# ScalarE evaluates to the end of a unit, and the last group gets all PSUM banks and both engines

## The chip, the cores and the metric

The kernel runs on one core of one Trainium2 chip. The time is the device time of one launch, in microseconds (us). Before the change it was 7317.06 us, the median of three runs (7311.98 to 7319.36); the profiled execution spans 7306.6 us.

The engines are called PE (TensorE, matrix products; PEld is its weight load), DVE (VectorE), ACT (ScalarE), POOL (GpSimd) and SP (SyncE, which here issues nearly all transfers). A matrix product goes into PSUM, in tiles of 128 x 512 fp32 values, and DVE or ACT takes it out; that is called an eviction here.

## The reference

The input `x` is 16 images of 32 channels, 128 x 128. Four residual layers follow each other, each on a group normalisation `_gn` of its input:

```python
x = x + L0(gn(x))    # a diagonal LSTM over the image
x = x + L1(gn(x))    # an adder convolution on quantised values
x = x + L2(gn(x))    # Hartley modes: transform, mix 32 x 32 modes, transform back
x = x + L3(gn(x))    # an edge-detecting encoder and decoder, multiplied with its input
```

Layer 1 is the one of the unit stage. With 8-bit quantised input `qx` and weights `qw` (3 x 3, 32 channels in and out) it computes a sum of absolute differences:

```python
patches = conv_general_dilated_patches(qx, (3, 3), (1, 1), [(1, 1), (1, 1)])
out = lax.map(lambda wk: -jnp.sum(jnp.abs(pr - wk[None, :, None]), axis=1), wf)
```

Layer 3 is the one of the end. Five edge operators are normalised over the image; then come conv1 (3 x 3, 160 to 32 channels), pooling to 64 x 64, conv2, pooling to 32 x 32, conv3, pooling to 16 x 16, conv4, and three steps of "upsample by 2, then 3 x 3 convolution" back to 128 x 128; the result is multiplied with the layer's input.

## The kernel before

**Three parts.** `stage0` does layer 0. `rest` (L438) does all others: class `Differences` does layer 1 for each image, class `After` does layers 2 and 3 in groups of four images (0 to 3). Work of `After` on images that are ready is woven into the loop of `Differences`. What is left of it when that loop ends, and the whole of group 3, runs in `drain` (L403).

**The unit.** `Differences.run` (L610) goes over 32 units: 16 images, two halves of 64 rows. The identity |a - b| = 2 max(a - b, 0) - (a - b) splits a unit into 72 evaluations of max(q - w, 0), one for each pair of a weight slot and a tap, over 128 partitions x 8192 values (8320 where the tap needs no shift), and a linear part (`linear`, L594). An evaluation is one instruction, on DVE (L684, into `d_dve`, three buffers) or on ACT (L681, into `d_act`, two buffers). PE then sums each result with 16 matrix products (`sums`, L581, products in L586) into four accumulators `acc1`, each a PSUM tile.

**Which engine evaluates.** For each evaluation the loop keeps planned times in `weave`: DVE_US = 2.36, ACT_US = 7.15. It computes when DVE and when ACT would end the evaluation, given their buffers, and takes ACT if that is at most 0.5 later than DVE. The last four evaluations of a unit, `i >= 68`, are always DVE's.

**The end of a unit.** At `i == 71` all sums not yet issued are issued. In the next unit the accumulators are replaced only after two DVE evaluations have been put in: then `finish` (L563) empties the old four (four instructions of L567, with the residual added, four of statistics, L569), and the new unit's sums may start. Four PSUM tiles belong to the units and four to the woven work.

**The woven work.** `After.work` is a generator. It yields planned PE time, and `Weave.advance` lets it run in PE's gaps up to the time when the next sum is due. Evictions and transfers that come later are put off by `later` and run when planned time has passed. In the loop of `Differences` the written order is kept on each engine (`keep_order`). In `drain` it isn't: the framework's scheduler orders the instructions there, by their written order and its own view of what is ready.

**The drain.** Two weaves run: the one that still has the rest of group 2, and one for group 3. The one with the smaller planned time goes next. Each has a pool of four PSUM tiles, `b_ps` and `c_ps`. When group 2 is done, group 3 goes on alone, with its four tiles.

**A round.** In `After` a round is a set of four accumulators (`acc`, L904), the products into all four, and four evictions. `spread` (L1539) writes an eviction as four instructions for 32 partitions each (`blk` counts the accumulators), all on the engine that its caller names: DVE for the pooled layers, conv4 and the first upsampling, ACT for conv1's output and the second upsampling. Lines: conv1 L1607, conv2 to conv4 L1455, upsampling L822 with edge terms in L847.

**The last layer.** `last` (L1652) goes over four units of 32 rows, two rounds each: DVE makes `s` (L1735) and multiplies it with the residual `xr` (L1698, two buffers), ACT subtracts a mean (`done`, L1708), then four transfers store the unit (L1714) and four reload `xr` for the unit after the next (L1677). The store is put off by 14 planned us, the reload by 10 more.

Of the kernel before, what the change touches and what calls it, by code (L numbers as in the profile page):

```python
# [7 lines left out]
F32 = mybir.dt.float32  # L8
# [291 lines left out]
class Weave:  # L300
# [10 lines left out]
    def __init__(self, work):  # L311
        self.work, self.pending = work, None
        self.pe = self.dve = self.act = self.now = self.base = 0.0
        self.until = self.ready = 0.0
        self.draining = False
        self.finished, self.count, self.put_off, self.for_act, self.ends = -1, 0, [], [], {}

    def later(self, us, step):
# [84 lines left out]
def drain(*weaves):  # L403

    live = list(weaves)
    for w in live:
        w.draining = True
    while live:
        w = min(live, key=lambda w: w.now)
        us = w.step()  # L410
        w.now = max(w.now + (us or 0.0), w.until)
        w.due(float("inf") if us is None else w.now)
        if us is None:
            live.remove(w)


def keep_order(nc, tc, start):
# [13 lines left out]


DVE_US, ACT_US, PE_US = 2.36, 7.15, 1.0
SLACK, CLOCK = 3.0, 1.0
SUMMED = ("summed",)


def rest(nc, tc, cst, sel16, bias, m1, r1, a, d, out):  # L438


    with ExitStack() as ctx:
        sm = ctx.enter_context(tc.tile_pool(name="s1_sm", bufs=1))
        stat = sm.tile([128, B, 8, 6], F32, name="stat2")
        with tc.tile_pool(name="s1_ps0", bufs=2, space=PSUM) as ps:
            first = Differences(nc, sm, ps, cst, sel16, m1, r1, a["adder_w"], d, stat)
        bg = ctx.enter_context(tc.tile_pool(name="b_ps", bufs=4, space=PSUM))
        after = After(nc, tc, "left", sm, bg, cst, bias, a, d, stat, out)
        weave = after.weave = Weave(after.work(range(NG - 1)))
        start = len(nc.cur_bb.bb.instructions)
        with ExitStack() as front:  # L450
            first.run(tc, front, weave)
        keep_order(nc, tc, start)

        end = copy.copy(after)
        end.side, end.ps = "right", ctx.enter_context(tc.tile_pool(name="c_ps", bufs=4, space=PSUM))
        end.weave = Weave(end.work([NG - 1]))
        end.weave.now = end.weave.base = weave.now
        end.weave.finished = B - 1
        drain(weave, end.weave)


class Differences:
# [97 lines left out]
            self.nc.sync.dma_start(xr[i], jc_rows(self.d["x1"], b, half, 8 * i, 8))  # L560
        return xr

    def finish(self, b, half, acc, xr):  # L563
        nc = self.nc
        v = [xr[k // 2][:, 512 * (k % 2) : 512 * (k % 2) + 512] for k in range(4)]
        for k in range(4):
            nc.vector.scalar_tensor_tensor(v[k], acc[k], self.sumw, v[k], ALU.subtract, ALU.add)  # L567
        for k in range(4):
            nc.vector.bn_stats(self.stat[:, b, 4 * half + k, :], v[k])  # L569

        def store():
            for i in range(2):
                nc.sync.dma_start(jc_rows(self.d["x2"], b, half, 8 * i, 8), xr[i])
            if half:
                self.weave.finished = b

        start = max(self.weave.dve, self.weave.pe)
        self.weave.pe, self.weave.dve = start + 2.6, start + 5.6
        self.weave.later(max(self.weave.dve - self.weave.base, 0.0) + 0.5, store)
# [30 lines left out]
    def run(self, tc, ctx, weave):  # L610
        nc, R, P = self.nc, self.R, self.P
# [6 lines left out]
        with tc.tile_pool(name="s1_x0", bufs=4, side="right") as pool:  # L618
            xq = [self.unquantised(0, i, pool) for i in range(4)]
            for i in range(4):  # L620
                self.scaled(0, xq[i])
                self.quantise(0, i, xq[i])
                weave.due(float("inf"))
        before, following = None, self.loaded(0, 0)

        free, count = {True: [0.0] * 2, False: [0.0] * 3}, {True: 0, False: 0}
        for b in range(B):
            for half in range(2):
                q, acc = following, None
                late, xq, summed = [], {}, 0  # L630

                def sums(until, last):

                    nonlocal summed
                    while late and (min(late)[0] <= until or last):
                        end, n, act, t = min(late)
                        late.remove((end, n, act, t))
                        self.sums(acc, t, n, not summed, last and not late)
                        summed += 1
                        weave.pe = max(weave.pe, end + 0.2) + PE_US  # L640
                        free[act].append(weave.pe)

                for i in range(72):
                    if not acc and sum(not v[2] for v in late) == 2:

                        if before:
                            self.finish(*before)
                        acc = [ps.tile([128, 512], F32, name="acc1") for _ in range(4)]
                        sums(weave.dve, False)
                    if i % 4 == 0 and 24 <= i < 60:  # L650
                        self.linear(acc, q, i // 4 - 6)
                    if i == 8 and (b, half) != (B - 1, 1):
                        following = self.loaded(b + half, 1 - half)
                    if i == 40:
                        xr = self.residual(b, half)
                    if half == 0 and b + 1 < B:
                        k = (i - 6) // 15
                        if 0 <= k < 4 and (i - 6) % 15 == 0:
                            xq[k] = self.unquantised(b + 1, k)
                        k = (i - 16) // 15  # L660
                        if 0 <= k < 4 and (i - 16) % 15 == 0:
                            self.scaled(b + 1, xq[k])
                        k = (i - 26) // 15
                        if 0 <= k < 4 and (i - 26) % 15 == 0:
                            self.quantise(b + 1, k, xq[k])
                    tap = i % 9
                    kh, kw = tap // 3, tap % 3
                    ends = {
                        act: max(weave.act if act else weave.dve, free[act][count[act]]) + (ACT_US if act else DVE_US)
                        for act in (True, False)  # L670
                        if count[act] < len(free[act])
                    }
                    act = False not in ends or (True in ends and i < 68 and ends[True] <= ends[False] + 0.5)
                    t = dp.tile([128, R, P], F16, name="d_act" if act else "d_dve", bufs=2 if act else 3)

                    src = q[:, kh : kh + R, :] if kw == 1 else q[:, kh : kh + R, kw : kw + W]
                    dst = t if kw == 1 else t[:, :, :W]
                    late.append((ends[act], i, act, t))
                    count[act] += 1
                    if act:  # L680
                        nc.scalar.activation(dst, src, AF.Relu, bias=self.neg[:, i : i + 1])  # L681
                        weave.act = ends[act]
                    else:
                        nc.vector.tensor_scalar(dst, src, self.qw[:, i : i + 1], 0.0, ALU.subtract, ALU.max)  # L684
                        weave.dve = ends[act]
                    if acc and (not act or i == 71):
                        sums(weave.dve, i == 71)
                    made = sum(not v[2] for v in late)
                    if acc:
                        weave.advance(min([v[0] for v in late] + [weave.dve + DVE_US]))  # L690
                    else:
                        weave.advance(weave.dve + (2 - made) * DVE_US + (2.6 if before else 0.0))
                before = b, half, acc, xr
        self.finish(*before)
        weave.due(float("inf"))


# [178 lines left out]
class After:  # L876


    def __init__(self, nc, tc, side, sm, ps, cst, bias, a, d, stat, out):
        self.nc, self.tc, self.side, self.ps, self.cst, self.bias = nc, tc, side, ps, cst, bias  # L880
        self.a, self.d, self.stat, self.out = a, d, stat, out
        store = [d["up"][i] for i in range(3)]
        self.up5 = Composed(nc, sm, a, "deconv1", "conv5", bias[:, 7:8], bias[:, 4:5], store[0])
        self.up6 = Composed(nc, sm, a, "deconv2", "conv6", bias[:, 8:9], bias[:, 5:6], store[1])
# [17 lines left out]
                    yield from self.last(g)  # L902

    def acc(self):  # L904
        return self.ps.tile([128, 512], F32, name="acc")

    def prepare(self):

# [627 lines left out]
    def spread(self, dst, src, blk, b, engine):  # L1536

        nc, weave = self.nc, self.weave
        for j in range(4):  # L1539
            d, s = dst(slice(32 * blk, 32 * blk + 32), j), src[32 * j : 32 * j + 32]  # L1540
            bj = b[32 * j : 32 * j + 32]
            if engine is nc.vector:
                nc.vector.tensor_scalar(d, s, bj, None, ALU.add)
                weave.dve += 0.3
            else:
                nc.scalar.activation(d, s, AF.Identity, bias=bj)  # L1546
                weave.act += 0.45
# [115 lines left out]
    def last(self, g):  # L1663

        nc, tc, cst, weave = self.nc, self.tc, self.cst, self.weave
        with self.pool("l_y") as yp, self.pool("l_x", 2) as xp:
# [39 lines left out]
            def done(x, unit):  # L1706
                for blk in range(4):
                    nc.scalar.activation(x[:, blk], x[:, blk], AF.Identity, bias=mean[:, blk : blk + 1])  # L1708
                weave.act += 4.4
                following[unit] = weave.later(14.0, lambda: store(x, unit))  # L1710

            def store(x, unit):
                for j in range(4):
# [200 lines left out]
```

## Time and profile before

| us | span | PE | DVE | ACT |
|---|---|---|---|---|
| whole | 7306.6 | 5566.3 (76%) | 5855.4 (80%) | 5318.0 (73%) |
| unit stage, 920 to 5945 | 5025 | 3857.0 | 4738.2 | 4588.6 |
| drain, two groups, 5945 to 7055 | 1110 | 902.7 | 361.2 | 248.9 |
| drain, last group, 7055 to 7307 | 252 | 196.0 | 82.3 | 47.3 |

| group of instructions | count | mean ns |
|---|---|---|
| ACT evaluation, L681 | 599 | 7141 |
| DVE evaluation, L684 | 1705 | 2360 |
| PE sum of a DVE evaluation, L586, one product | 27280 | 415 |

The columns PE, DVE and ACT are busy times. Products of PE overlap and their ends are modelled, so a busy PE isn't a full one. A wait is shown as "engine line <- what released it". A share of the granted PE clock below 1 means that PE ran part of the stretch at a lower clock. The borders 5945 and 7055 were chosen from the order of time: at 5945 the last statistics of the units end, and about 7055 the last products of group 3's conv1 begin.

### The profile page before, as it was taken

Reading aid. Unit: us, or ns where it says so; the run is one execution under the profiler, and the core shown is the slowest. Engines: PE = TensorE matmul, PEld = TensorE weight load, DVE = VectorE, ACT = ScalarE, POOL = GpSimd, SP = SyncE. Lnnn points to the kernel's source line nnn. Section 1 sums busy time; section 2 is a strip of 40 time slices with the busy share of each in tenths; the row PEclk is TensorE's granted clock in tenths of the full one; section 3 lists DMA queues with packets and bytes.
Section 4 is the critical chain, followed back from the end, with each engine's and each line's share of the span. In section 5 each row is a group of like instructions: output and inputs, shape, how many; then the busy total and the mean of one; then the engine's idle time right before and its main releaser. Section 6 shows DMA issues by size and latency. Waiting matters only on the chain. (4 is left out here: it accounts for less than half of the span.)

```text
span 7306.6 us, 258155 instructions
## 1 busy us (share of the span) xinstructions
PE 5566.3 (76%) x121132; PEld 3000.3 (41%) x121132; DVE 5855.4 (80%) x7046; ACT 5318.0 (73%) x3116; POOL 36.3 (0%) x31
## 2 busy tenths in 40 slices
PE   4778566666677687998777676999788777798887
PEld 3665322222244343333344333333334456445544
DVE  7787599999999999999898889999899982423232
ACT  2556399989999998998988878999898941131312
POOL 0000000000000000000000000000000000000000
PEclk9899788888888898998888887999887876799996
DMA  8654111111133442211342243111233245531324
GB/s 312 227 195 164 65 63 55 48 58 51 40 96 106 136 115 78 62 43 50 78 134 94 79 139 111 58 55 50 57 100 100 98 138 151 156 102 46 81 62 96
DMA packets 374268, 721.67 MB, mean 99 GB/s; under 512 B 50896, under 2 KB 219856, under 8 KB 362320
## 3 DMA queue, kind: packets, MB, share of 16 engines
q1 hardware_dynamic: 372768, 704.58, 31.3%
q8 instruction: 948, 15.53, 0.9%
q14 instruction: 120, 0.98, 0.0%
q10 hardware_dynamic: 432, 0.57, 0.0%
HBM read 507.21 MB, written 164.32 MB: 92 GB/s over the span
## 5 line engine op out<-in xcount | busy, mean ns | idle before, releaser
L681 ACT ACTIVATE d_act<-q,neg 128x8192 f16<-128x8192 f16 (+1 forms) x599 | 4237.0, 7141 | 383.8 <-PE acc L586 330.8
L684 DVE TENSOR_SCALAR d_dve<-q,qw 128x8192 f16<-128x8192 f16 (+1 forms) x1705 | 3929.7, 2360 | 187.4 <-PE acc L586 144.1
L586 PE MATMUL acc<-d_dve,sel 128*32 128x512 f16 x27280 | 1957.5, 415 | 750.4 <-DVE d_dve L684 741.5
L586 PEld LDWEIGHTS <-sel 128*32 128x32 f16 x36864 | 1045.7, 103 | 2521.4 <-issue 1862.7
L1607 PE MATMUL acc<-xp,wf 32*32 32x512 f32 x25600 | 1052.9, 625 | 50.7 <-issue 29.9
L586 PE MATMUL acc<-d_act,sel 128*32 128x512 f16 x9584 | 759.4, 439 | 346.2 <-ACT d_act L681 276.9
L1607 PEld LDWEIGHTS acc<-xp,wf 32*32 32x32 f32 x25600 | 415.9, 105 | 428.5 <-issue 344.9
L1252 ACT ACTIVATE xp<-xp,shift,stats 128x1280 f32<-128x1280 f32 (+1 forms) x128 | 182.5, 1434 | 434.5 <-DMA xp<-x_d 298.3
L1546 ACT ACTIVATE y<-pooled,b 32x128 f32<-32x128 f32 x512 | 204.7, 400 | 398.8 <-DVE pooled L1532 392.1
L207 PE MATMUL pg<-h,wb 64*64 64x20 f32 (+15 forms) x4096 | 393.7, 318 | 105.0 <-DVE h L256 64.0
L822 PE MATMUL acc<-y,u_conv 32*32 32x256 f32 (+1 forms) x9728 | 409.9, 491 | 82.6 <-issue 41.0
L244 ACT ACTIVATE gt<-pg,bias 128x20 f32<-128x20 f32 (+15 forms) x1024 | 316.6, 375 | 78.8 <-PE pg L207 72.0
L207 PE MATMUL pg<-e,wb 64*64 64x20 f32 (+15 forms) x4096 | 351.1, 313 | 17.2 <-DVE e L260 6.0
L207 PEld LDWEIGHTS pg<-h,wb 64*64 64x64 f32 x4096 | 245.4, 152 | 140.9 <-DVE h L256 90.5
L207 PE MATMUL pg<-xn,wb 64*64 64x28 f32 (+61 forms) x4096 | 283.9, 302 | 11.6 <-ACT gt L244 3.9
L822 PEld LDWEIGHTS acc<-y,u_conv 32*32 32x32 f32 x9728 | 193.8, 115 | 233.3 <-issue 152.8
L207 PEld LDWEIGHTS pg<-e,wb 64*64 64x64 f32 x4096 | 249.3, 154 | 93.0 <-DVE e L260 63.9
L1292 PE MATMUL acc<-xp 32*64 32x204 f32 (+3 forms) x8576 | 245.6, 351 | 31.5 <-ACT xp L1258 23.4
L255 ACT ACTIVATE th<-c 128x20 f32<-128x20 f32 (+15 forms) x256 | 81.3, 320 | 236.1 <-DVE c L253 234.5
L1735 DVE TENSOR_SCALAR s<-acc,l_ms,l_one 128x512 f32<-128x512 f32 x128 | 102.7, 829 | 168.8 <-PE acc L822 168.8
L207 PEld LDWEIGHTS pg<-xn,wb 64*64 64x64 f32 x4096 | 216.0, 153 | 36.6 <-ACT gt L244 10.9
L1292 PEld LDWEIGHTS acc<-xp 32*64 32x64 f32 (+1 forms) x8576 | 173.3, 137 | 123.5 <-issue 93.3
(203 smaller groups left out, 4173.4 us busy)
## 6 DMA issues: line engine op xcount, KB each, us to landing
xr<-x_d SPq DMA_DIRECT2D x192, 512.0 KB
xp<-x_d SPq DMA_DIRECT2D x112, 640.0 KB
q<-q_d SPq DMA_DIRECT2D x32, 2145.0 KB
x_d<-xr SPq DMA_DIRECT2D x128, 512.0 KB
x_in<-in_x_dram SPq DMA_DIRECT2D x16, 2048.0 KB
res<-in_x_dram SPq DMA_DIRECT2D x64, 512.0 KB
xn<-in_xs_dram SPq DMA_DIRECT2D x64, 512.0 KB
xn<-xn SPq DMA_DIRECT2D x128, 256.0 KB
```

The source lines that it names most:

```text
L207: nc.tensor.matmul(bank[c][q][64 * pair : 64 * pair + 64, :, :width], wb[half, 4 * kind + KIND[q]].rearrange("p b o -> p (b o)"), v[half], ...
L244: nc.scalar.activation(gt[:, q, :, :n], bank[c][q][:, :, :n], AF.Tanh if q == G else AF.Sigmoid, bias=bias[:, KIND[q] : KIND[q] + 1],)
L255: nc.scalar.activation(th[:, :, :n], cell, AF.Tanh)
L586: self.nc.tensor.matmul(acc[k][32 * j : 32 * j + 32, :], self.sel16[:, i // 9, :], d[:, row : row + 4, c : c + W], start=first, stop=last,)
L681: nc.scalar.activation(dst, src, AF.Relu, bias=self.neg[:, i : i + 1])
L684: nc.vector.tensor_scalar(dst, src, self.qw[:, i : i + 1], 0.0, ALU.subtract, ALU.max)
L822: nc.tensor.matmul(acc[blk][32 * j : 32 * j + 32, o : o + rows * n], t[part, 4 * par + tap, :], src[part, top : top + rows, left : left + ...
L1252: nc.scalar.activation(v, v, AF.Identity, bias=self.shift3, scale=self.stats3[:, 1])
L1292: nc.tensor.matmul(gram[blk][j : j + width, at : at + n], xp[part, l, 2 + j : 2 + j + width], xp[part, rows, j : j + width + 4], start=sta ...
L1546: nc.scalar.activation(d, s, AF.Identity, bias=bj)
L1607: nc.tensor.matmul(acc[blk][32 * j : 32 * j + 32, :], tap_of("all", tap)[rows], xp[rows, 4 * j + kh : 4 * j + kh + 4, kw : kw + W], start= ...
L1735: nc.vector.tensor_scalar(s.rearrange("p r w b -> p b r w"), acc[blk].rearrange("p (b r w) -> p b r w", b=2, w=64), istd[:, blk : blk + 1] ...
```

## The change

There are four edits.

1. **ACT to the end of a unit.** The rule `i < 68` goes. In the last four evaluations ACT is taken if it ends at most `(71 - i) * DVE_US + LATE` after DVE would end this one, that is at most 1.5 us after DVE's planned end of the unit.
2. **Last sums in the next unit.** Sums that aren't due at the unit's end stay in the unit's record and are issued in the next unit, in order of their planned ends; what is left is issued just before `finish`.
3. **All banks and both engines for the last group alone.** When one weave is left, its rounds take their accumulators in turn from its own pool and from the other's (`spare`), and `spread` puts even blocks on DVE and odd ones on ACT.
4. **Earlier stores.** When alone, a store of the last layer is put off by 4 instead of 14 planned us.

Edit 1 uses ACT where it had no evaluation left in its unit; edit 2 makes room for an ACT evaluation that ends after DVE's last; edit 3 lets a round start while the one before is emptied; edit 4 frees the residual's buffer sooner.

```diff
@@ drain
         if us is None:
             live.remove(w)
+            for w in live:
+                w.alone = True
...
@@ rest
         end.side, end.ps = "right", ctx.enter_context(tc.tile_pool(name="c_ps", bufs=4, space=PSUM))
+        end.spare = bg
...
@@ Differences.run
+        def sums(unit, until, last=False):
+
+            late = unit["late"]
+            while late and (min(late)[0] <= until or last):
+                end, n, act, t = min(late)
+                late.remove((end, n, act, t))
+                self.sums(unit["acc"], t, n, unit["summed"] == 0, unit["summed"] == 71)
+                unit["summed"] += 1
+                weave.pe = max(weave.pe, end + 0.2) + PE_US
+                free[act].append(weave.pe)
...
-                    if not acc and sum(not v[2] for v in late) == 2:
+                    if not unit["acc"] and sum(not v[2] for v in unit["late"]) == 2:
 
                         if before:
-                            self.finish(*before)
-                        acc = [ps.tile([128, 512], F32, name="acc1") for _ in range(4)]
-                        sums(weave.dve, False)
+                            sums(before, weave.dve, True)
+                            self.finish(**before)
+                        unit["acc"] = [ps.tile([128, 512], F32, name="acc1") for _ in range(4)]
+                        sums(unit, weave.dve)
...
-                    act = False not in ends or (True in ends and i < 68 and ends[True] <= ends[False] + 0.5)
+                    act = False not in ends or (
+                        True in ends and ends[True] <= ends[False] + (0.5 if i < 68 else (71 - i) * DVE_US + LATE)
+                    )
...
-                    if acc and (not act or i == 71):
-                        sums(weave.dve, i == 71)
-                    made = sum(not v[2] for v in late)
-                    if acc:
-                        weave.advance(min([v[0] for v in late] + [weave.dve + DVE_US]))
+                    current = unit if unit["acc"] else before
+                    if current and not act:
+                        sums(current, weave.dve)
+                    due = [v[0] for v in current["late"]] if current else []
+                    if unit["acc"]:
+                        due.append(weave.dve + DVE_US)
                     else:
-                        weave.advance(weave.dve + (2 - made) * DVE_US + (2.6 if before else 0.0))
-                before = b, half, acc, xr
-        self.finish(*before)
+                        made = sum(not v[2] for v in unit["late"])
+                        due.append(weave.dve + (2 - made) * DVE_US + (2.6 if before else 0.0))
+                    weave.advance(min(due))
+                before = unit
+        sums(before, weave.dve, True)
+        self.finish(**before)
...
@@ After
     def acc(self):
-        return self.ps.tile([128, 512], F32, name="acc")
+
+        self.banks += 1
+        ps = self.spare if self.weave.alone and self.banks // 4 % 2 else self.ps
+        return ps.tile([128, 512], F32, name="acc")
...
@@ After.spread
-            if engine is nc.vector:
+            if blk % 2 == 0 if weave.alone else engine is nc.vector:
...
@@ After.last, done
-                following[unit] = weave.later(14.0, lambda: store(x, unit))
+                following[unit] = weave.later(4.0 if weave.alone else 14.0, lambda: store(x, unit))
```

## The prediction

> **What bounds the kernel now.** I read four views: busy time by stretch, the waits of each engine inside a stretch, the order of time at one unit's end, and the chain of waits at the very end. First the stretches. The columns are length, then busy us of PE, PE weight load, DVE, ACT, POOL, then granted PE clock, DMA share and GB/s. The first row is the stage of the 32 units, the second the part of the rest in which two groups run together, the third the part that the last group runs by itself; the last two rows split the third.
>
> ```profile
> 920.00:5945.00 5025.00, 3857.02 (x78070) 1801.66 (x78069) 4738.17 (x3740) 4588.63 (x1211) 28.82 (x15) 0.88 0.26 79
> 5945.00:7055.00 1110.00, 902.71 (x26062) 611.12 (x26068) 361.19 (x904) 248.86 (x488) 5.11 (x9) 0.83 0.41 115
> 7055.00:7307.00 252.00, 195.97 (x4707) 114.31 (x4694) 82.34 (x187) 47.30 (x64) 0.00 (x0) 0.69 0.34 78
> 7055.00:7168.00 113.00, 92.41 (x2083) 47.17 (x2070) 36.56 (x123) 22.14 (x38) 0.00 (x0) 0.77 0.11 26
> 7168.00:7307.00 139.00, 103.56 (x2624) 67.14 (x2624) 45.78 (x64) 25.16 (x27) 0.00 (x0) 0.64 0.53 121
> ```
>
> In the first row DVE is busy 94.3% and ACT 91.3% of 5025 us: the two share one pool of evaluations, and together they are the bound; PE has a quarter free. In the third row nobody is full: PE is busy 78% at a clock of 0.69, so latency binds there. Next, what ACT and DVE wait for in the unit stage (us in total, times, longest):
>
> ```profile
> ACT d_act L681 <- PE acc L586: 330.8, 61, 20.2
> ...
> DVE d_dve L684 <- PE acc L586: 144.1, 88, 26.7
> ```
>
> ACT's largest wait is for PE to give back one of its two `d_act` buffers. Where it lies is seen at the end of a unit (the one that ends near 1195 us), ACT, then DVE, then PE:
>
> ```profile
> 1169.28 21.36 ACT L681 ACTIVATE d_act<-q,neg 128x8320 f16<-128x8320 f16 x3 [1.53 <-PE acc L586]
> 1203.80 7.12 ACT L681 ACTIVATE d_act<-q,neg 128x8192 f16<-128x8192 f16 x1 [13.16 <-PE acc L586]
> ...
> 1200.31 2.72 DVE L567 SCALAR_TENSOR_TENSOR xr<-acc,sumw,xr 128x512 f32<-128x512 f32 x4
> 1202.95 2.46 DVE L569 BATCH_NORM_STATS2 stat<-xr 128x6 f32<-128x512 f32 x4
> ...
> 1195.31 1.48 PE L586 MATMUL acc<-d_dve,sel 128*32 128x512 f16 x16 [0.47 <-DVE d_dve L684]
> 1201.11 4.30 PE L586 MATMUL acc<-d_act,sel 128*32 128x512 f16 x32 [4.31 <-DVE xr L567]
> ```
>
> ACT has no more work of the old unit (its last four evaluations are DVE's by rule), runs two of the new unit ahead, and then stands for 13.16 us: their sums need the accumulators, which DVE empties (L567) only after two evaluations of the new unit. DVE never stops meanwhile. The idle ACT time is therefore beside a full DVE.
>
> The last view is the chain at the end, where the last group is alone:
>
> ```profile
> 7095.72 3.94 DMA w_conv<-in_conv_dram
> ...
> 7163.79 4.49 DMA u_conv<-up_d
> ```
>
> ```profile
> PE acc L822 <- issue: 16.2, 7, 4.2
> PE acc L822 <- DVE s L1735: 6.9, 8, 1.3
> PE acc L1455 <- DMA w_conv<-in_conv_dram: 4.3, 1, 4.3
> ...
> PE acc L822 <- ACT y L1546: 3.0, 1, 3.0
> ```
>
> The first two rows are pieces of that chain (start, us); the second fence has PE's waits in that stretch. PE stops at each round for an engine that is emptying its four banks (`DVE s`, `ACT y`), and at two layer changes for a weight load.
>
> **What the Trainium skill says.** "TensorE: Matmul & The Clock Gate", section "Part 1: The HAM clock gate": after an idle window of some 3.4 us the PE clock goes to half, and returns after a busy one. The trace agrees: inside one round the clock was 0.50 at 7190 to 7193.5 us, just after a wait, and 1.00 at 7197 to 7200.5. So small PE gaps in the tail cost twice. "PSUM — Partial Sum Buffer", section "Specifications (TRN2)": eight banks of 512 fp32 values. One `acc` tile is thus a bank and a round takes four; the trace fits, since rounds wait for evictions. The same page, "PSUM bank collisions raise a hardware error": different engines may work on different banks at once; before the change DVE and ACT never share one round's evictions, so no row shows it.
>
> **The change, part by part.**
>
> *More evaluations on ACT.* Counting the instructions of both programs: `d_act` 599 to 625, `d_dve` 1705 to 1679, that is 26 moved, at most one or two in each of the 32 units. By the page's means DVE loses 26 x 2.36 = 61 us and ACT gains 26 x 7.14 = 186 us. ACT has 331 us of waits for buffers to put it in, mostly at unit ends, so ACT goes to 4775 busy of some 4975, 96%. DVE is at 94% and waits little, so its saving should mostly come off the stage. Bounds: 61 us if all of it does; 0 if a nearly full ACT makes PE, and behind it DVE's three buffers, wait for late `d_act` (that wait is 276.9 us of PE now). I take 0.8, 49 us.
>
> *Last sums moved into the next unit.* PE gets the old unit's last sums in order of their planned ends, between background work, and they are flushed before `finish`, which stays behind DVE's second new evaluation. This adds a possible wait: PE on a late `d_act`, then `finish` on DVE, with all of DVE's evaluations queued behind it. DVE's two new evaluations give 2 x 2.36 = 4.7 us of cover, the rule lets ACT end 1.5 us after DVE by plan, and one unit's sums last about 1 us, so 2 us are spare; besides, ACT was ahead in the trace (idle from 1190.6, DVE's last old evaluation ended after 1195). I cost it at nothing, with 7.14 - 2 = 5.1 us a unit as the worst end, an evaluation late by its whole length.
>
> *Eight banks when alone.* PE's order in the tail is all but unchanged, but a round no longer waits for the round before. Conv2's two rounds: 1.2 us standing before the first, and pieces of 1.29 and 0.70 us of `pooled` in the chain before and in the second, 3.2 together. The second upsampling: 3.0 us standing, and its second round took 13.6 us for what the first did in 10.9 plus its own pacing, 3 more: 6. The last eight rounds: 6.9 us of waits plus 2 of second pieces: 9.
>
> *Both engines on an eviction.* 16 instructions of 0.48 us on DVE (7.7) become 8 there beside 8 on ACT (between its 0.40 for 128 and its 0.72 for 512 columns): 3.7 saved ahead of the second upsampling. Conv3 to conv4 and conv4 to upsampling (4.0 and 4.5 us now) save 2 each. Conv2 to conv3 and the start of the last layer save nothing: the weight loads of 3.9 and 4.5 us end last.
>
> *Stores 4 instead of 14 us later.* In the DMA queue of the changed program the reload of unit 2 now stands behind one store of unit 1, and that of unit 3 still behind one store of unit 2, so the queue waits for ACT before each. One reload is later, the other some us earlier: 3 us saved, bounds -5 and +8.
>
> *Clock.* With 26 us of gaps gone from a stretch of 196 busy us at 0.69, I expect about 0.8: 196 x (1 - 0.69 / 0.8) = 27 us, but the last eight rounds are then held by DVE (5.7 us a round) and the reloads, and by unexplained 3 to 4 us stops ("issue", 16.2 us) that stay. I take 10, bounds 0 and 27.
>
> Tail: 3.2 + 6 + 9 + 3.7 + 4 + 3 + 10 = 39 us, between 15 and 62. The two-group stretch has the same work in nearly the same PE order: 0, give or take 10.
>
> Sum: 7317 - 49 - 39 = 7229 us.
>
> **Rivals.**
> 1. *The stage gives back its saving* (ACT becomes the bound, PE waits for it). For: ACT at 96%, and PE already waits 277 us for `d_act`. Against: at a unit's end it is ACT that waits. Time: 7317 - 39 = 7278.
> 2. *The tail is held by transfers*, since a reload waits behind a store: tail only 15. For: 512 KB pieces in one queue, DMA share 0.53. Against: the gaps of the first 113 us have no transfer in them but two. Time: 7317 - 55 - 15 = 7247.
> 3. *Everything comes off and lucky background stops too*: DVE stood 22.6 us once for `xr`, 21.7 for `xm`, 26.7 for PE; the background moves a little. 61 + 62 + 15 gives 7179.
> 4. *Slower*: the flush at each unit's start holds DVE 5.1 us, 32 x 5.1 = 163, less 61 and 39: 7317 + 63 = 7380. For: DVE is strictly behind `finish`. Against: the 13 us of ACT's lead.
>
> **How the numbers follow.** Forecast 0.55, rival 1 0.17, rival 2 0.13, rival 3 0.07, rival 4 0.08. The range leaves out rival 4 and the outer ends: 7180 to 7285. Faster than 7302 takes the first four and a small loss for unlucky stops: 0.88; within 0.2%: 0.05; slower: 0.07.
>
> **What the profile after would show.** Right: `d_act` waits for PE cut from 331 to about 150 us, DVE's busy time in the stage 60 us less, the stage near 4975 us; from conv2 to the end some 210 us at a clock near 0.8, with no `DVE s` or `ACT y` wait of PE. Wrong: PE's wait for `d_act` well over 277, or `xr` L567 waiting for PE at unit starts, or a stall of `xr` L1698 on a reload over 10 us. What could spoil the number most is a chance stop of 20 to 40 us in the woven background.

## The result and the profile after

| | median us | runs from to |
|---|---|---|
| before | 7318.21 | 7311.98 to 7320.48 (4) |
| after | 7269.60 | 7259.99 to 7280.27 (4) |

The ratio is 0.9935, with a 95% interval of 0.9918 to 0.9953: 48.6 us faster. The forecast was 7229, so some 40 us of the expected 88 did not come. (Two line numbers given above are off by a few: in the listing `spread` starts at L1536 and `last` at L1663.)

First the stretches, to see where the time went. The columns are as in the prediction: length, busy us of PE, PE weight load, DVE, ACT and POOL, granted PE clock, DMA share, GB/s. The borders are the same events as before: the stage ends near 5930, and group 3's conv2 begins at 7065.

```profile
920.00:5930.00 5010.00, 3831.07 (x78030) 1796.49 (x78033) 4681.19 (x3711) 4770.36 (x1237) 41.83 (x15) 0.88 0.26 79
5930.00:7065.00 1135.00, 913.07 (x26416) 611.73 (x26408) 361.14 (x907) 247.69 (x488) 5.10 (x9) 0.82 0.41 113
7065.00:7258.00 193.00, 121.97 (x4391) 85.41 (x4382) 82.93 (x171) 48.32 (x80) 0.00 (x0) 0.79 0.41 98
```

Before, the same last stretch began at 7067 (this row replaces the one from 7055, which holds some of conv1):

```profile
7067.00:7306.00 239.00, 185.83 (x4386) 108.29 (x4386) 81.47 (x183) 47.30 (x64) 0.00 (x0) 0.68 0.35 79
```

The last stretch went from 239 to 193 us: 46 us, as much as the whole change. The stage, from its first to its last evaluation, went only from 5020.6 to 5009.2, and the two-group stretch from 1126.5 to 1135.9, which takes most of that back. Each of these is one profile: kernels run later, whose stage is the old one, show it at 5015.7 to 5032.7, so a few us either way are chance.

Yet the evaluations did move. Two groups of the changed kernel's page, then the waits of ACT, DVE and PE in its stage (us in total, times, longest):

```profile
L689 ACT ACTIVATE d_act<-q,neg 128x8192 f16<-128x8192 f16 (+1 forms) x625 | 4419.7, 7142 | 207.9 <-PE acc L590 157.4
L692 DVE TENSOR_SCALAR d_dve<-q,qw 128x8192 f16<-128x8192 f16 (+1 forms) x1679 | 3873.8, 2362 | 211.9 <-PE acc L590 168.6
```

```profile
ACT d_act L689 <- PE acc L590: 157.4, 43, 26.7
```

```profile
DVE d_dve L692 <- PE acc L590: 168.6, 102, 22.1
DVE wf L1435 <- DMA v<-fold_d: 43.8, 3, 34.4
```

```profile
PE acc L590 <- ACT d_act L689: 395.3, 220, 11.2
```

ACT's wait fell from 330.8 to 157.4, as forecast. But DVE's waits grew where nobody looked for it: a fold table (`v`) that was late by 34.4 us once, against 8.6 in all before. And PE's wait for ACT rose from 276.9 to 395.3. Adding up DVE's time from its first evaluation to its last, in us:

| DVE in the stage | evaluations | other work | idle | sum |
|---|---|---|---|---|
| before | 3893.6 | 840.5 | 286.5 | 5020.6 |
| after | 3837.1 | 842.7 | 328.8 | 5008.6 |

56.5 us less evaluation, 42.3 us more standing. By blocks of four units (a unit ends where `finish` starts to empty its accumulators, the last one with its last evaluation), six of the eight blocks became 45 us shorter together; units 12 to 15 became 15.7 and units 20 to 23 became 17.6 us longer. The second of these has the two long stops. Here is the first of them, in order of time: the DMA queue of SP, then ACT, PE and DVE.

```profile
4323.81 1.06 SPq L557 DMA_DIRECT2D q<-q_d  x1
4324.97 41.13 SPq L1262 DMA_DIRECT2D xp<-x_d  x3
```

```profile
4367.65 1.46 ACT L1268 ACTIVATE xp<-xp,shift,stats 128x1280 f32<-128x1280 f32 x1 [25.18 <-DMA xp<-x_d]
```

```profile
4369.40 1.06 PE L1308 MATMUL acc<-xp 32*64 32x204 f32 x16 [22.53 <-ACT xp L1274]
```

```profile
4372.34 2.35 DVE L692 TENSOR_SCALAR d_dve<-q,qw 128x8192 f16<-128x8192 f16 x1 [22.14 <-PE acc L590]
```

Read from the end: DVE stands for its buffers, PE for the input rows that a woven group needs, ACT for their load, and that load (640 KB, the first of the three that the second row merges) was issued right behind `q`, the evaluation input of the next unit (2145 KB). In the middle of it the core does almost nothing:

```profile
4348.00:4366.00 18.00, 0.00 (x0) 0.00 (x0) 2.20 (x1) 0.00 (x0) 0.00 (x0) 0.53 0.33 105
```

The DMA share of 0.33 is the clue: a transfer is what all wait for, and on average the DMA engines are busy a third of the time. The second stop has the same shape, with the fold table (720 KB) behind a `q`:

```profile
4513.12 0.56 SPq L557 DMA_DIRECT2D q<-q_d  x1
4516.40 46.58 SPq L1420 DMA_DIRECT2D v<-fold_d  x4
```

```profile
4560.91 1.72 DVE L1435 SCALAR_TENSOR_TENSOR wf<-v,ops,wf 128x1440 f32<-128x1440 f32 x1 [34.36 <-DMA v<-fold_d]
```

"DMA: Bandwidth & Descriptors" of the Trainium skill, section "Rules for kernel authors", says why: the outermost dimension of a transfer's access pattern caps how many DMA engines it uses, and a leading zero-stride broadcast of c copies confines it to at most c. `q` is loaded by one transfer whose source begins with `[0, 4]`, four copies: four of 16 engines. The section "Queues, rings and completion order" adds that one issuing queue has a ring on each DMA engine, consumed in order. By that, a load behind `q` has most of its share done early and waits for the part on the four busy engines. The trace agrees. At the start of the stage before, where almost nothing but `q` moves, the DMA share is 0.25 (a row below). And the semaphore updates that tell of a landing show the four late parts: of the 16 updates of the load issued at 4324.97, twelve had come by 4332.5 and the last four came from 4360.1 to 4367.6, while the four of `q` came from 4358.2 to 4365.7. For the fold table issued at 4516.40 it is twelve by 4523.9 and four from 4553.9 to 4560.8, with those of `q` from 4552.4 to 4559.2.

### The profile page after: what moved, and what is told of

Read it like the earlier page. It is cut to its first block, busy times and chain, and to the rows that moved or that the text cites. A ratio compares the mean times of both kernels' runs of the same rounds, so it can differ in the third digit from the quotient of the medians.

```text
span 7258.2 us, 258133 instructions
## 1 busy us (share of the span) xinstructions
PE 5476.8 (75%) x121132; PEld 2966.0 (41%) x121132; DVE 5799.8 (80%) x7004; ACT 5499.6 (76%) x3158; POOL 49.4 (1%) x31
## 3 DMA queue, kind: packets, MB, share of 16 engines
q1 hardware_dynamic: 372768, 704.58, 31.7%
## 5 line engine op out<-in xcount | busy, mean ns | idle before, releaser
L689 ACT ACTIVATE d_act<-q,neg 128x8192 f16<-128x8192 f16 (+1 forms) x625 | 4419.7, 7142 | 207.9 <-PE acc L590 157.4
L692 DVE TENSOR_SCALAR d_dve<-q,qw 128x8192 f16<-128x8192 f16 (+1 forms) x1679 | 3873.8, 2362 | 211.9 <-PE acc L590 168.6
L590 PEld LDWEIGHTS <-sel 128*32 128x32 f16 x36864 | 1063.0, 103 | 2526.9 <-issue 1926.2
L590 PE MATMUL acc<-d_act,sel 128*32 128x512 f16 x10000 | 783.5, 437 | 423.4 <-ACT d_act L689 395.3
L834 PE MATMUL acc<-y,u_conv 32*32 32x256 f32 (+1 forms) x9728 | 342.0, 459 | 66.1 <-issue 46.8
L834 PEld LDWEIGHTS acc<-y,u_conv 32*32 32x32 f32 x9728 | 169.6, 109 | 180.3 <-issue 119.7
```

The source lines that it names most:

```text
L590: self.nc.tensor.matmul(acc[k][32 * j : 32 * j + 32, :], self.sel16[:, i // 9, :], d[:, row : row + 4, c : c + W], start=first, stop=last,)
L834: nc.tensor.matmul(acc[blk][32 * j : 32 * j + 32, o : o + rows * n], t[part, 4 * par + tap, :], src[part, top : top + rows, left : left + ...
```

## The experiments

My theory: all of the gain is the tail's; the stage edits are sound, but their moved evaluations meet stops behind `q`. First rival: a nearly full ACT (the prediction's rival 1). Second rival: the sums moved into the next unit hold DVE. Times are medians of kernels that ran beside the kernel before, and each ratio is to that. There were three such groups of runs, in which the kernel before took 7318.92, 7312.47 and 7320.21 us, so times of different groups are compared by their ratios.

**The parts by themselves.** Edits 3 and 4 alone on the kernel before:

```diff
+            for w in live:
+                w.alone = True
...
+        ps = self.spare if self.weave.alone and self.banks // 4 % 2 else self.ps
...
-            if engine is nc.vector:
+            if blk % 2 == 0 if weave.alone else engine is nc.vector:
...
-                following[unit] = weave.later(14.0, lambda: store(x, unit))
+                following[unit] = weave.later(4.0 if weave.alone else 14.0, lambda: store(x, unit))
```

> The kernel before with the tail's edits alone (all banks, both engines, earlier stores for the last group; 599 evaluations on ACT as before). Theory 1, all of the gain is the tail's: 48 us less than before, about 7269, the same as the changed kernel. Theory 2, the unit stage gives half as the prediction had it (profile after: stage 12 us shorter) and the rest is the tail: 36 us less, about 7281.

Measured: 7264.88 us beside 7318.92, ratio 0.9922 (0.9908 to 0.9935), 54 us faster. The tail is 194.3 us long in its profile, as in the changed kernel.

Edits 1 and 2 alone, the changed kernel without its flag:

```diff
-            for w in live:
-                w.alone = True
```

> The changed kernel without the tail's edits (625 evaluations on ACT, last sums moved). Theory 1: no difference from before that can be told, 7317 within 10 us, although DVE does 26 evaluations (61 us) less. Theory 2: 12 us or more less, about 7305. The prediction's own number for this part was 49 less, 7268.

Measured: 7313.72, ratio 0.9996 (0.9987 to 1.0006). Nothing that can be measured: stage 5017.8, two-group stretch 1133.4 (7 us longer than before), tail 238.8 as before. The two long stops are there again, at the same places (17.2 and 31.7 us of DVE). The theory's first half stands: 54 and 5 us, against 48.6 for the whole change, agree within their intervals.

Edit 2 alone, the old rule back in the kernel above:

```diff
-                        True in ends and ends[True] <= ends[False] + (0.5 if i < 68 else (71 - i) * DVE_US + LATE)
+                        True in ends and i < 68 and ends[True] <= ends[False] + 0.5
```

> The last sums moved into the next unit, with the old rule that gives the last four evaluations to DVE (599 on ACT), without the tail's edits. If moving the sums costs waits at unit starts: 10 to 30 us more than before. If it is free, as the prediction had it: within 10 us of before.

Measured: 7319.62, ratio 1.0002 (0.9993 to 1.0011). Moving the last sums costs nothing as long as the last four evaluations are DVE's. With ACT's late ones among them this run can't tell. In the stage of the changed kernel the emptying of the old accumulators (`DVE xr L571`) waited for PE once, 1.1 us, which leaves little to the second rival.

Edit 1 alone: the new rule, while all last sums are still issued at the unit's end (622 evaluations on ACT instead of 625):

```diff
-                    act = False not in ends or (True in ends and i < 68 and ends[True] <= ends[False] + 0.5)
+                    act = False not in ends or (
+                        True in ends and ends[True] <= ends[False] + (0.5 if i < 68 else (71 - i) * DVE_US + LATE)
+                    )
```

> The new rule for ACT in the last four evaluations (622 on ACT), with the last sums still flushed at the unit's end, without the tail's edits. If a nearly full ACT is what eats the saving: about as the stage's edits together, 7305 to 7317, PE's wait for d_act 390 us or more. If the moved sums eat it: better than the stage's edits together by 10 us or more.

Measured: 7225.79, ratio 0.9875 (0.986 to 0.9889), 93 us faster. That is more than the 54 us or so of DVE time that was moved, so something else must have come with it. The stage is 4910.3 us long, 110 less than before: 53 us less of evaluations, 13 less of DVE's other work, and 44 less of idle time (242.3 us, where the changed kernel has 328.8 and the kernel before 286.5). Some of it was only put off: 448 woven products moved behind the stage's end, and what follows the stage became 29 us longer. And PE waits for ACT longer than before the change (276.9) or after it (395.3):

```profile
PE acc L587 <- ACT d_act L684: 442.4, 249, 9.7
```

So a large wait of PE for `d_act` goes together here with the shorter stage, which speaks against the first rival as the whole story. Whether the flush is better than moved sums, or its background happened to fall well, this run can't tell; the last pair below does.

**The load of `q`.** Four transfers of 32 partitions, one for each copy, instead of one; first in the kernel before:

```diff
-        self.nc.sync.dma_start(q, bass.AP(q_d.tensor, first, [[0, 4], [(H + 2) * P, C], [1, (self.R + 2) * P]]))
+        for j in range(4):
+            self.nc.sync.dma_start(
+                q[32 * j : 32 * j + 32], bass.AP(q_d.tensor, first, [[(H + 2) * P, C], [1, (self.R + 2) * P]])
+            )
```

> The kernel before with the load of q (2145 KB, four copies of 32 partitions in one transfer, seen at a DMA share of 0.25 for 22 to 42 us) issued as four transfers, one for each copy. Theory C (the stage's saving is lost in stops of woven work whose load sits behind that transfer): the stops of 20 us and more in units 12 to 27 go, the stage falls by 40 us or more, about 7270. Theory D (a nearly full ACT takes the saving, transfers are beside the point): within 10 us of before, 7319.

Measured: 7250.23 beside 7312.47, ratio 0.9912 (0.9897 to 0.9926), 62 us faster. The 42 us ahead of the old stage start, before the edit and with it (columns as for the stretches above):

```profile
878.00:920.00 42.00, 0.29 (x8) 0.30 (x9) 0.58 (x4) 0.00 (x0) 0.00 (x0) 0.50 0.25 71
```

```profile
878.00:920.00 42.00, 15.27 (x274) 7.02 (x276) 25.23 (x16) 24.22 (x4) 0.00 (x0) 0.72 0.66 142
```

With one transfer the core waits for `q` at a DMA share of 0.25; with four the share is 0.66 and the first evaluation starts at 895.7 instead of 920.2. Of the 48 us between the two profiles, 25 are this earlier start and 27 the stage (5020.6 to 4993.3), where 40 or more had been expected; the tail is 3 longer. DVE's waits with the edit, from the start of the stage:

```profile
DVE d_dve L687 <- PE acc L589: 177.6, 105, 9.5
DVE d_dve L687 <- DMA q<-q_d: 16.3, 1, 16.3
```

Past its start, no wait of DVE in the stage exceeds 10 us; before, single ones took 21.7, 22.6 and 26.7.

The same edit in the changed kernel:

> The changed kernel with the load of q in four transfers. Theory C: the stage loses its stops and the 26 moved evaluations show: the stage is 40 to 60 us shorter than that of the kernel before with the same load, and the whole 90 to 110 us less than that one, about 7170. Theory D: about 7265 as the changed kernel, and PE still waits 390 us for d_act with the stage near 5010.

Measured: 7194.24, ratio 0.9838 (0.9819 to 0.9857), 71 us less than the changed kernel by the ratios. Here is the same view:

```profile
DVE d_dve L695 <- PE acc L593: 200.6, 117, 9.5
DVE d_dve L695 <- DMA q<-q_d: 16.2, 1, 16.2
DVE wf L1438 <- DMA v<-fold_d: 12.7, 3, 9.6
```

The 22.1 and the 34.4 are gone, and so is the loss in units 20 to 23 (693.6 us, now 639.3). That the long stops come from `q` is shown.

That they are what ate the stage's saving is not. The kernel before had such stops too and gained 62 us when they went, the changed kernel 71. With `q` in four transfers the change is worth 56 us (7250.23 to 7194.24), where it was worth 48.6 with one, and where the theory had 90 to 110. In the profiles the stage is now 30 us shorter through the change (4993.3 to 4963.4), where it was 11 shorter and where 40 to 60 were expected; the two-group stretch is 13.5 longer (1126.9 to 1140.4). So the stops explain 7 us of what was missed in the whole time, which can't be told from nothing (each of the two differences is uncertain by more than 10 us), or some 19 of the stage. The tail, 45.7 us shorter in these two profiles, is again most of the change.

Of the 54 us of evaluations moved, 30 show in the stage; 21 come back as DVE's idle time (257.8 to 279.1), which its waits for PE's sums account for (177.6 to 200.6). PE in turn waits more for ACT (251.3 to 359.8): that part is the first rival's mechanism, though not shown by taking it away, for which a third `d_act` buffer would be needed; that was not tried.

**Combinations.** The new rule with the flush, edits 3 and 4 added, and then the four transfers too:

```diff
+LATE = 1.5
...
-                    act = False not in ends or (True in ends and i < 68 and ends[True] <= ends[False] + 0.5)
+                    act = False not in ends or (
+                        True in ends and ends[True] <= ends[False] + (0.5 if i < 68 else (71 - i) * DVE_US + LATE)
+                    )
```

> The new ACT rule with the sums flushed at the unit's end as before, and the tail's edits. If the two gains add up (93 and 54 us, measured one at a time): about 7172. If the gain of the ACT rule alone was partly a different cut between stage and drain that the tail takes back: 7180 to 7200.

> The same with the load of q in four transfers. Theory C: moving the sums was never the cost, so this comes within 20 us of the changed kernel with four transfers (7170). If flushing at the unit's end is better by itself: 50 us or more below that one.

Measured: 7188.08, ratio 0.9831 (0.9816 to 0.9847), and 7149.43, ratio 0.9771 (0.9755 to 0.9787). The two gains do not add up: the first version is 124 us faster than the kernel before, where the new rule and the tail by themselves gave 93 and 54. The second is the fastest version run: 163 us below the kernel before in the same comparison, and 120 below the changed kernel. It is 45 us below the one with moved sums, where one theory had 20 at most and the other 50 at least.

**Edits 3 and 4 taken apart.** Edit 3's banks alone, then its engines alone, both with the stores put off by 14 us as before (the cuts shown are against the kernel with edits 3 and 4):

```diff
-            if blk % 2 == 0 if weave.alone else engine is nc.vector:
+            if engine is nc.vector:
```

> The kernel before with one tail edit: rounds of the last group alone take banks from both pools in turn. The tail as a whole gave 54 us. By the prediction's terms (3.2 at conv2, 6 at the second upsampling, 9 at the last layer's rounds, most of 10 for the clock): 20 to 30 us less than before. If the waits removed pass to the next dependence: under 10.

```diff
-        ps = self.spare if self.weave.alone and self.banks // 4 % 2 else self.ps
-        return ps.tile([128, 512], F32, name="acc")
+        return self.ps.tile([128, 512], F32, name="acc")
```

> The kernel before with one tail edit: evictions of the last group alone are shared by DVE and ACT. By the prediction's terms (3.7 and 4 us for the layers with one round, and a part of the second upsampling's 6 that the banks would also give): 8 to 14 us less than before.

Measured beside 7320.21: banks 7277.67, ratio 0.9941 (0.9928 to 0.9953), 42.5 us; engines 7303.32, ratio 0.9976 (0.9966 to 0.9985), 17 us. Together they would be 59, both with the stores gave 54. In the profiles the tail is 202.7 us with the banks and 227.6 with the engines, 36.5 and 11.6 less than before, and 44.9 less with both and the earlier stores. The stores were not run by themselves, but nothing that they gain is to be seen. The upsampling products of the tail, with the banks and then with the engines (before: 139.0 us busy, further below):

```profile
L825 PE MATMUL acc<-y,u_conv 32*32 32x256 f32 (+1 forms) x2432 | 94.4, 515 | 40.9 <-issue 33.6 <-DMA u_conv<-up_d 3.7 <-ACT y L1552 3.6
```

```profile
L824 PE MATMUL acc<-y,u_conv 32*32 32x256 f32 (+1 forms) x2432 | 120.4, 592 | 27.7 <-issue 13.7 <-ACT y L1548 7.2 <-DVE s L1737 6.7
```

**Is the flush better, or its background luckier?** A change of the plan that adds no work to the program: the factor by which the weave counts the woven work's PE time, 1.03 for 1.0. It was put into both kernels with `q` in four transfers, the one with moved sums and the one with the flush:

```diff
-SLACK, CLOCK = 3.0, 1.0
+SLACK, CLOCK = 3.0, 1.03
```

> The changed kernel with q in four transfers, and the plan's PE time for woven work 3% longer (CLOCK 1.03), which moves pieces of woven work to other places and nothing else (621 evaluations on ACT instead of 625). Measured without it: 7194. If where pieces happen to fall is worth tens of us: anywhere from 7150 to 7230. If it is worth little: 7184 to 7204.

> The new ACT rule with the flush at the unit's end, the tail's edits and q in four transfers, with the plan's PE time for woven work 3% longer in the same way. Measured without it: 7149, 45 us below the version with moved sums. If the flush is better by itself: again 30 to 60 us below the moved sums with the same longer plan. If that difference was where pieces fell: less than 15 us, or the other way round.

Measured beside 7320.21:

| last sums | factor 1.0 | factor 1.03 |
|---|---|---|
| moved | 7194.24 | 7219.96 (0.9861, 0.9847 to 0.9874) |
| flushed | 7149.43 | 7232.96 (0.9879, 0.9865 to 0.9892) |

The column for 1.0 is from the group of runs beside 7312.47. The order turns round: the flush led by 45 us and now trails by 13. By the ratios, the plan's factor alone moved the two by 17 and 79 us. The change is not as neutral as it was meant to be: with the factor less woven work fits into the stage, 1952 products less with moved sums and 887 less with the flush, and the first kernel has 621 evaluations on ACT instead of 625. So work passes from the stage to what follows it. The stages went from 4963.4 to 4932.9 us (moved) and from 4894.5 to 4936.1 (flushed), while from the stage's end to the last transfer issued it takes 1383.6 and 1385.9 us, against 1329.8 and 1348.9 without it. Where the woven work falls, inside the stage or behind it, is thus worth tens of us, and the lead of the flush is not shown to be the flush's. The same caution holds for the 93 us of edit 1 alone, and for the 40 us by which the forecast missed.

## Why the prediction was right in the tail and wrong in the stage

**26 evaluations moved, 61 us off DVE: right.** 1705 to 1679, and 56.5 us less by the trace. ACT's wait for PE came to 157.4 us, against "about 150". That the last sums cost nothing by themselves was right too (1.0002).

**"I take 0.8, 49 us": the step that failed.** It held that DVE's saving comes off the stage because DVE "is at 94% and waits little". 11 us came, and with the two-group stretch nothing that can be measured (0.9996). The stage was forecast near 4975 and took 5009. What stands in place of the 0.8 is shown in part. The long stops behind `q` are one piece: with them six blocks' 45 us lose 33 again, and without them the stage keeps 30 of 54 us, a factor of 0.55. But they cost the kernel before almost as much, and taking them away made the change worth only 7 us more. The other piece is DVE waiting for PE's sums and PE for ACT's evaluations, rival 1 in a milder form; its time, 7278, was the nearest to 7269.6. Why the two-group stretch then takes back most of what is left stays open. The prediction had named "a chance stop of 20 to 40 us in the woven background" as what could spoil it most. It took these stops for chance; they were in the profile of before (41.2 us for the first `q`, single stops of DVE of 21.7, 22.6 and 26.7 that began while a later one was loading), with one cause that could be named, and they came back at the same places in a second run of the stage edits.

**"The two-group stretch: 0, give or take 10": right**, at +9. It has the same products (26 383 before, as the rows from 5945 and 7055 less the row from 7067 give, and 26 416), so it was slower, not longer by work. Some 3 us of the 9 are the border: the old accumulators begin to be emptied 0.8 us after the stage's last evaluation before, and 3.9 us after it now, since the last sums come later. The rest was not settled.

**The tail: mechanism right in the main, 39 us forecast, 46 in the trace, 54 by itself.** The mis-sized terms are the banks with the clock: 3.2 + 6 + 9 and 10 for the clock make 28, the run with banks alone gave 42.5 (36.5 in the tail of its profile). The engines were put at 3.7 + 4 and gave 17 (11.6 in the tail). The waits of PE in the tail after the change, then the upsampling products in both kernels, before first (busy us, mean ns; idle before):

```profile
PE acc L834 <- issue: 30.7, 14, 6.5
PE acc L859 <- issue: 7.6, 4, 4.0
PE acc L834 <- ACT y L1562: 4.3, 1, 4.3
PE acc L1471 <- DMA w_conv<-in_conv_dram: 4.0, 1, 4.0
```

```profile
L822 PE MATMUL acc<-y,u_conv 32*32 32x256 f32 (+1 forms) x2432 | 139.0, 588 | 27.4 <-issue 16.2 <-DVE s L1735 6.9 <-ACT y L1546 3.0
```

```profile
L834 PE MATMUL acc<-y,u_conv 32*32 32x256 f32 (+1 forms) x2432 | 84.3, 496 | 35.5 <-issue 30.7 <-ACT y L1562 4.3 <-DVE y L1559 0.4
```

`DVE s` no longer stops PE, as forecast, and one `ACT y` stop of 4.3 us is left. But the idle time ahead of these products did not fall: it rose by 8 us, because the "issue" stops grew. The gain is in the busy column: 2432 products took 54.7 us less. Part is the clock, 0.68 to 0.79: as an estimate 139.0 x (1 - 0.68 / 0.79) = 19 us of the 54.7, and 26 us of all 186 busy us in the tail, against the 10 taken and the 27 that the step had worked out and then cut. The rest lies inside a round. Both rounds here ran mostly at half clock (0.63 and 0.50); the first is before, the second after:

```profile
7202.13 6.12 PE L822 MATMUL acc<-y,u_conv 32*32 32x256 f32 x92 [0.93 <-DVE s L1735]
```

```profile
7206.40 2.96 PE L834 MATMUL acc<-y,u_conv 32*32 32x256 f32 x78 [6.48 <-issue]
```

That is 67 ns a product with four banks and 38 with eight. The start of a round ran at the pace at which banks came free, in pieces too short to show as a wait; the 0.93 us shown was only its first piece. That is how I read it. The runs of the parts support it: the products take 94.4 us with the banks alone and 120.4 with the engines alone, so most of the 54.7 us comes with the banks; but no run separates the pace at a round's start from the clock. The prediction had counted just the shown waits, 6.9 us plus 2. "TensorE: Matmul & The Clock Gate", section "A second HAM failure mode: psum-queue depth-cycling", describes such a loss, short stops between groups of products while banks are cycled, with the clock going back and forth; the trace fits it: in the tail the granted clock is either 0.50 or 1.00, before and after, and changes after 3.4 us or a multiple of it. The prediction's reading that the half clock at 7190 came "just after a wait" is not exact: it began at 7186.6, beside a stop of 3.04 us, and the next at 7203.7, beside one of 0.93. So the clock here fell beside single stops that were shorter than the idle window of some 3.4 us that it quotes.

**Stores and reloads: order right, size wrong.** The queue after:

```profile
7173.01 21.23 SPq L1730 DMA_DIRECT2D out_dram<-xr  x5
7194.43 3.45 SPq L1693 DMA_DIRECT2D xr<-x_d  x4
7197.92 22.73 SPq L1730 DMA_DIRECT2D out_dram<-xr  x4
7220.76 3.65 SPq L1693 DMA_DIRECT2D xr<-x_d  x4
```

```profile
DVE xr L1714 <- DMA out_dram<-xr: 23.4, 2, 11.9
```

Four stores and one of the next unit go ahead of the first reload, as said. The residual's stops came to 23.4 us, and 11.9 is over the 10 named as a sign of error; it was 5.3 before. It is not edit 4's doing: with the banks alone and late stores they are 18.7 us, longest 12.0. Faster rounds reach the reload sooner; that part of the banks' gain stops there is my reading, and no run shows it.

**Rivals 2 and 4** did not come: the tail gave 46 to 54 us, not 15, and no unit was held by its flush (1.1 us in all). The time measured lies inside the range, on the side of rival 1, and in part by luck: the stage's term came to nothing, and a tail worth 54 instead of 39 made up for some of it.

## What to carry to other kernels

Before pricing work moved between two engines that share a pool, look at the longest single stops, not only the sum of busy time: here a few stops of 20 to 40 us with a DMA share near a quarter had one cause, and it cost more (62 us) than the change brought. Then test whether removing it changes what the edit is worth, and not only the time: here it hardly did. A change that shifts woven work by a little moved this kernel by tens of us, so test an edit with a second plan of the same work, and count what work passes from one stretch to another, before believing its size. In a stretch bound by latency, the waits counted from the profile (18 us) were less than what more PSUM banks brought (36.5 us in the tail, the clock's part included), since products ran slowly without a wait being shown.

## What the runs showed of the hardware that was not expected

- One load of 2145 KB with a source of four leading copies held the DMA share at 0.25 for some 40 us, and kept a part of the loads of 640 and 720 KB behind it from landing until it was done (12 of 16 landing updates after 7.5 us, the last four after 43 and 44 us); four transfers of the same bytes took 62 us off the kernel before.
- PE's "issue" stops in the tail rose from 19.7 us to 39.5 us (single ones up to 6.5), as the products themselves got faster. What they wait for the profile doesn't show, and no run here tells.
